# Two-layer graph attention on one core: layer 0 in a hand-made order, layer 1's rows turned by VectorE alone

## The chip, the cores and the metric

The kernel runs on one NeuronCore of a Trainium2 chip. The metric is the device time of one execution in microseconds (us); lower is better. The median of three runs of the kernel before is 937.08 us, from 936.54 to 939.74.

The names of the engines in the profile: PE is TensorE (PEld its weight loads), DVE is VectorE, ACT is ScalarE, POOL is GpSimd, SP is SyncE, which here only issues DMAs. An engine name with a q (SPq, ACTq) is that engine's sequencer issuing a DMA.

## What is computed

Two residual layers over 4096 nodes of 512 features, with a dense 4096 x 4096 adjacency matrix of positive weights (zero where there is no edge):

```python
# layer 0: attention inside graphs of 128 nodes (32 graphs); adj is both b and edge_encoding
h = relu(layernorm(x))
q, k, v = h @ Wq.T + bq, h @ Wk.T + bk, h @ Wv.T + bv
a = where(same_graph, q @ k.T / sqrt(512), 0)
scores = (a + adj + adj) * where(same_graph, 1, -1e6)
x = x + (softmax(scores) * same_graph) @ v

# layer 1: graph attention, 8 heads of 64, over all edges of adj
h = relu(layernorm(x))
mx = einsum('nf,hfd->hnd', h, W)
logits = (mx . a_origin)[:, :, None] + (mx . a_dst)[:, None, :]
attn = softmax(where(adj > 0, logits, -big))
x = x + concat_heads(attn @ mx)
```

In layer 1 the a_origin term cancels in the softmax, so a head's output is a sum over the neighbours of exp(t_j) * mx_j divided by the sum of exp(t_j). The kernel works on 32 tiles of 128 rows.

## The kernel before

It has four stages.

The start (`fold`) multiplies Wq and Wk into one matrix (`m_sb`), with the bias terms folded in: it loads and transposes both weights, spreads the biases with small matmuls, and forms the products.

Layer 0 goes through 16 groups of two tiles. Its loads of the adjacency matrix are half tiles of 1 MB in seven buffers; each half is turned into mask bytes by VectorE (stored in `a_d` for layer 1) and summed with exponentials by ScalarE. Eight tiles of layer 1 are projected in its gaps, with `prepare_on`:

```python
def begin1():                                  # a row tile of layer 1: load, normalise
    row = sb2.tile([P, D], F32, name="row1")
    nc.sync.dma_start(row, x1_d[len(rows1)])
    norm(row, row)
    rows1.append(row)

def turned1(row):                              # four TensorE transposes, relu out of PSUM
    hT = sb2.tile([P, KC, P], F32, name="hT1")
    relu_T(ps_t, row, hT)
    return hT
...
def relu_T(ps_pool, hn, dst):
    pt = ps_pool.tile([P, KC, P], F32, name="pt")
    for k in range(KC):
        nc.tensor.transpose(pt[:, k, :], hn[:, ts(k, P)], ident)
    nc.scalar.activation(dst, pt, AF.Relu)
...
for g in range(NG):                            # layer 0, cut
    ...
    s = scores(g, hT, gT, r, *look)
    prepare_on(last)
    if not last:
        ngT = queries(nhT)
    sT = turned(s)
    prepare_on(3 <= g and g % 2)
    ...
    for t in range(G):
        look_on(t)                             # adjacency halves of the next group
        if not last and t == 0:
            nvs.append(values(nhT, t))
        attend(sT, vs[t], g, t)
        if not last and t:
            nvs.append(values(nhT, t))
    ...
    if g + 2 < NG:
        nhT, hns = turned0(g + 2)
        nr = row_terms(hns)
```

The order on each engine is left to the framework in this stage. The lines of the profile in it: scores L519, queries L461, the turning of scores L538, values L473, attend L546 (with VectorE's x1, L548), transposes L136, projection of layer 1 L264, mask bytes L146, adjacency exponentials L496.

The middle stage projects layer 1's tiles 8 to 31, in an order that the program gives for all engines but TensorE. Tiles 8 to 15 are still turned by TensorE. Tiles 16 to 31 are turned by VectorE: a stream transpose turns 32 x 32 blocks, four tiles are collected in `blocks`, stored to DRAM and loaded back in another arrangement, which completes the turning:

```python
def turn(i):
    c, b = divmod(i, BY)
    if b == 0:
        blocks[c] = sb4.tile([P, P // B, KC, BY, B], F32, name="blocks")   # two buffers
    nc.vector.transpose(
        blocks[c][:, :, :, b], rows[i].rearrange("p (k q f) -> p q k f", k=KC, f=B)
    )
    if b == BY - 1:
        nc.sync.dma_start(hT_d[c], blocks[c].rearrange("p q k b r -> p q (k b r)"))

def move(c):
    hT = sb5.tile([P, P // B, KC, P], F32, name="hT4")
    for q in range(P // B):
        nc.sync.dma_start(hT[ts(q, B)]..., hT_d[c, :, q]...)
    for u in range(BY):
        hTs[c * BY + u] = hT[:, u]
```

The last stage (L315) sums, for each of the 32 tiles, over all neighbours: 96 matmuls of 128 x 128 by 348 columns for a tile. The change does not alter it.

Of the kernel before, what the change touches and what calls it, by code (L numbers as in the profile page):

```python
# [9 lines left out]
F32 = mybir.dt.float32  # L10
# [15 lines left out]
H = 8  # L26
# [18 lines left out]
MIXED = NT // 2  # L45
AHEAD = 8
# [7 lines left out]
def kernel(  # L54
# [43 lines left out]
    nc.scalar.dma_start(bq_sb, bq)  # L98
    bk_sb = const.tile([P, KC], F32, name="bk_sb")
    nc.scalar.dma_start(bk_sb, bk)  # L100
# [7 lines left out]
    def load_adj(pool, k):  # L108

        a = pool.tile([P, NH], F32, name="a")  # L110
        nc.sync.dma_start(a, adj[ts(k // 2, P), ts(k % 2, NH)])
        return a
# [26 lines left out]
    def mask_bytes(a8, a, h):  # L139

        half = ts(h, NW // 2)
        a8v = a8.rearrange("p (u c q b) -> p u c b q", c=NW, q=B, b=BY)[:, :, half]
        order = ("p (c b u q) -> p u c b q", "p (c u b q) -> p u c b q")[h]
        av = a.rearrange(order, c=NW // 2, b=BY, q=B)
        for u in range(P // B):
            nc.vector.tensor_scalar(  # L146
                a8v[:, u], av[:, u], 0.0, None, ALU.is_gt, saturate=False
            )
# [10 lines left out]
    def load_w1(pool, tmp):  # L159
# [3 lines left out]
        a_sb = tmp.tile([P, D], F32, name="a_sb", bufs=1)  # L163
        nc.sync.dma_start(a_sb, a_dst.to_broadcast([P, D]))
        for k in range(KC):
            wa = tmp.tile([P, D], F32, name="wa", bufs=1)
            nc.vector.tensor_tensor(wa, w[:, k, :D], a_sb, ALU.mult)
            nc.vector.tensor_reduce(
                w[:, k, D:], wa.rearrange("p (h d) -> p h d", d=HD), AX.X, ALU.add
            )  # L170
        return w

    def fold(sb, tmp, work, ps_t, ps_p, loads, first):
# [3 lines left out]
        wkT_sb = load_weight(tmp, wkT, "wkT_sb", KC, tag="lo")  # L177
        wqT_sb = load_weight(tmp, wqT, "wqT_sb", KC, tag="lo")
# [12 lines left out]

        nat = []
        for n, wT in enumerate((wkT_sb, wqT_sb)):
            w = tmp.tile([P, KC, D], F32, name=f"w{n}", tag="lo")
            for k in range(KC):
# [4 lines left out]
                if n == 0 and k == 0:  # L200
                    rows = [spread_bias(b) for b in (bk_sb, bq_sb)]
# [18 lines left out]
        for m in range(KC):  # L220
# [11 lines left out]
            if m == 3:  # L232
                first()
            pp = ps_p.tile([P, D], F32, name="pp")
            for k in range(KC):
                nc.tensor.matmul(
                    pp, wq[:, k, ts(m, P)], wk[:, k, :], start=(k == 0), stop=(k == KC - 1)
                )
            nc.scalar.mul(m_sb[:, m, :], pp, SCALE)  # L239
# [140 lines left out]
    with ExitStack() as straight:  # L380
# [4 lines left out]
        with ExitStack() as prep:  # L385
# [12 lines left out]
            rows1 = []  # L398

            def begin1():  # L400
                row = sb2.tile([P, D], F32, name="row1")
                nc.sync.dma_start(row, x1_d[len(rows1)])
                norm(row, row)
                rows1.append(row)

            def turned1(row):
                hT = sb2.tile([P, KC, P], F32, name="hT1")
                relu_T(ps_t, row, hT)
                return hT
# [13 lines left out]
            def prepare(i, hT, part):  # L423
                pm = project1(ps_p, hT, w1x)
                finish(weights(i, pm), pm, part)

            with (
                tc.tile_pool(name="adj0", bufs=AB, side="right") as ap,
# [4 lines left out]
                def turned0(g):  # L433

                    hT = sb.tile([P, KC, G * P], F32, name="hT")
                    hns = []
                    for t in range(G):
                        hn = sb.tile([P, D], F32, name="hn")
                        norm(xg[g][:, t, :], hn)
                        relu_T(ps_t, hn, hT[:, :, ts(t, P)])  # L440
                        hns.append(hn)
# [13 lines left out]
                def queries(hT):  # L455

                    gT = sb.tile([P, KC, G * P], F32, name="gT")
                    for m in range(KC):
# [8 lines left out]
                        )  # L467
                    return gT

                def values(hT, t):  # L470
# [6 lines left out]
                    nc.vector.tensor_add(v, pp, bv_sb)  # L477
                    return v

                def read(i, diag, sums):  # L480


                    a8 = sb.tile([P, N], FP8, name="a8", bufs=3)
                    n = 1
                    for h in range(2):
                        a, base = aa[2 * i + h], h * NH
                        mask_bytes(a8, a, h)
                        own = i * P - base
                        pieces = ((0, NH),)
                        if 0 <= own < NH:  # L490
                            nc.gpsimd.tensor_copy(diag, a[:, ds(own, P)])
                            pieces = ((0, own), (own + P, NH))
                        for c0, c1 in pieces:
                            if c0 < c1:
                                junk = sb.tile([P, NH], BF16, name="junk", bufs=1)
                                nc.scalar.activation(  # L496
                                    junk[:, c0:c1], a[:, c0:c1], AF.Exp, scale=2.0 * NEG,
                                    accum_out=sums[:, n : n + 1],
                                )
                                n += 1  # L500
                        if h:
                            nc.sync.dma_start(a_d[i], a8.bitcast(F32))
                        if 2 * i + h + AB < 2 * NT:
                            aa[2 * i + h + AB] = load_adj(ap, 2 * i + h + AB)
                    return n

                def seen():
                    return (
                        sb.tile([P, G, P], F32, name="diag", bufs=3),
# [4 lines left out]
                def scores(g, hT, gT, r, diag, sums, counts):  # L514
# [8 lines left out]
                    s = sb.tile([P, G, P], F32, name="s")  # L523
                    nc.vector.scalar_tensor_tensor(s, diag, 2.0, pss, ALU.mult, ALU.add)
                    for t in range(G):
# [3 lines left out]
                        )  # L529
                        rsum = rs_all[:, G * g + t : G * g + t + 1]  # L530
                        nc.vector.tensor_reduce(rsum, sums[t][:, : counts[t]], AX.X, ALU.add)
                        nc.vector.reciprocal(rsum, rsum)
                    return s

                def turned(s):
# [3 lines left out]
                    sT = sb.tile([P, G, P], F32, name="sT")  # L539
# [3 lines left out]
                def attend(sT, v, g, t):  # L543
                    i = G * g + t
                    po = ps_p.tile([P, D], F32, name="pp")
                    nc.tensor.matmul(po, sT[:, t, :], v, start=True, stop=True)  # L546
                    x1 = sb.tile([P, D], F32, name="x1")
# [12 lines left out]
                xg, aa = {}, {}  # L560
                first = []

                def loads():
                    load_pair(0)
                    first.append(load_weight(wp, wvT, "wv"))
                    nc.scalar.dma_start(bv_sb, bv.to_broadcast([P, D]))
                    for k in range(4):
                        aa[k] = load_adj(ap, k)
                    load_pair(1)
                    for k in range(4, AB):  # L570
                        aa[k] = load_adj(ap, k)

                m_sb, c_sb, u_sb, z_sb = fold(
                    wp, lo, sb, ps_t, ps_p, loads, lambda: first.extend(turned0(0))
                )
# [3 lines left out]
                look = seen()  # L579
                for t in range(G):  # L580
                    look[2].append(read(t, look[0][:, t, :], look[1][t]))
                gT = queries(hT)
                nhT, hns = turned0(1)
                nr = row_terms(hns)
                ahead = []
                for g in range(NG):
                    last = g + 1 == NG
                    if g + 2 < NG:
                        load_pair(g + 2)
                    if g == 1:  # L590
                        w1x = load_w1(pool1, sb)
                    nlook = seen()

                    def look_on(t):
                        if not last:
                            i = G * (g + 1) + t
                            nlook[2].append(read(i, nlook[0][:, t, :], nlook[1][t]))

                    def prepare_on(now):
                        if now:  # L600
                            i = len(ahead)
                            ahead.append(turned1(rows1[i]))
                            if i:
                                prepare(i - 1, ahead[i - 1], part_tile(lo, i - 1))

                    s = scores(g, hT, gT, r, *look)
                    prepare_on(last)
                    if last:
                        begin1()
                    if not last:  # L610
                        ngT = queries(nhT)
                    sT = turned(s)
                    prepare_on(3 <= g and g % 2)

                    for _ in range({2: 1, NG - 2: 1, NG - 1: 0}.get(g, int(3 <= g and g % 2))):
                        begin1()
                    nvs = []
                    for t in range(G):
                        look_on(t)
                        if not last and t == 0:  # L620
                            nvs.append(values(nhT, t))
                        attend(sT, vs[t], g, t)
                        prepare_on(last and t == 0)
                        if not last and t:
                            nvs.append(values(nhT, t))
                    if not last:
                        hT, r, gT, vs, look = nhT, nr, ngT, nvs, nlook
                    if g + 2 < NG:
                        nhT, hns = turned0(g + 2)
                        nr = row_terms(hns)  # L630

# [6 lines left out]
            sb5 = prep.enter_context(tc.tile_pool(name="sb5p", bufs=2, reuse_waits="tile"))  # L638
            begun = ExitStack()
            sb4 = begun.enter_context(  # L640
                tc.tile_pool(name="sb4p", bufs=2, side="right", reuse_waits="tile")
            )
            rows, of, blocks, hTs = {}, {}, {}, {}
# [469 lines left out]
```

## Time and profile before

| stage, us from the start | TensorE busy | VectorE busy | ScalarE busy | GpSimd busy | DMA engines' share |
|---|---|---|---|---|---|
| 0 to 29: start | 24.59 | 15.58 | 17.16 | 8.14 | 0.92 |
| 29 to 195: layer 0, first part | 165.78 | 125.98 | 113.99 | 38.00 | 0.93 |
| 195 to 212 | 16.86 | 10.88 | 9.95 | 4.93 | 0.93 |
| 212 to 340: layer 0, second part | 128.00 | 75.09 | 63.38 | 24.27 | 0.67 |
| 340 to 379: last group, first layer 1 tiles | 39.00 | 28.82 | 21.53 | 22.78 | 0.36 |
| 379 to 443: rest of the middle stage | 63.49 | 36.56 | 21.96 | 33.77 | 0.63 |
| 443 to 916: aggregation | 473.00 | 163.28 | 18.90 | 47.08 | 0.23 |
| 916 to 937: last tile and end | 15.15 | 6.04 | 1.25 | 1.48 | 0.14 |

A row is a stretch of the profiled execution, whose span is 936.6 us; each cell is how long the engine was busy in it. Matmuls are pipelined, so the profile's durations of single ones overlap; the time that a group of them takes is read from the start of the next group. Several DMA engines serve all queues; their share is the mean over 16.

### The profile page before, as it was taken

The numbers are of one execution on the slowest core, as the hardware profiler recorded it, in microseconds if no ns is written. First come the engines' busy times: TensorE is split into PE (matmuls) and PEld (weight loads), VectorE is DVE, ScalarE is ACT, GpSimd is POOL, SyncE is SP. The second block draws the span as 40 slices with busy tenths as digits, with TensorE's granted clock in tenths as the row PEclk, the third lists the DMA queues.
The fourth block names the chain that finished last, engine by engine and source line by source line (L and its number), as shares of the span: only waits on it lengthen the run. The fifth ranks groups of instructions, "written<-read, shape, count | busy, mean of one in ns | idle before, by whom it ended". The sixth has DMA issues, their size and how long they took to land.

```text
span 936.6 us, 13145 instructions
## 1 busy us (share of the span) xinstructions
PE 925.9 (99%) x4987; PEld 809.1 (86%) x4987; DVE 462.2 (49%) x992; ACT 268.1 (29%) x539; POOL 180.4 (19%) x344
## 2 busy tenths in 40 slices
PE   8999999999999999999999999999999999999997
PEld 5676677767677778888999999999999999999997
DVE  4678878777775447754463324242424233332412
ACT  4876576667672216532000000000000000000000
POOL 1311212331221116654101010110101010101010
PEclk9999999999999999999999999999999999999999
DMA  9999997989997114764123131312121222313111
GB/s 334 415 382 401 349 351 302 360 344 371 356 354 273 35 35 146 203 200 103 53 61 91 46 90 46 90 51 85 52 85 54 82 71 65 88 48 90 46 45 37
DMA packets 61062, 156.63 MB, mean 167 GB/s; under 512 B 6722, under 2 KB 23490, under 8 KB 52290
## 3 DMA queue, kind: packets, MB, share of 16 engines
q1 hardware_dynamic: 51058, 138.70, 42.9%
q10 hardware_dynamic: 9936, 17.05, 4.9%
q8 instruction: 40, 0.66, 0.3%
q14 instruction: 28, 0.23, 0.1%
HBM read 117.97 MB, written 37.75 MB: 166 GB/s over the span
## 4 chain that ended last, share of the span: by engine, by line
PE 94%; DMA 3%; ACT 2%; DVE 0%; SPq 0%; issue 0%; ACTq 0%
PE pg L315 51%; PE pp L264 12%; PE pp L461 11%; PE pp L473 11%; PE pp L546 3%; PE pss L519 3%; DMA a<-adj 2%; PE pt L136 2%; ACT junk L496 1%; PE pl L315 1%; DMA bv_sb<-bv 1%; PE pss L538 0%; ACT m_sb L239 0%; ACT gT L465 0%; DVE x L548 0%
## 5 line engine op out<-in xcount | busy, mean ns | idle before, releaser
L315 PE MATMUL pg<-part,ata 128*128 128x348 f32 (+1 forms) x1536 | 246.7, 321 | 0.0
L315 PEld LDWEIGHTS pg<-part,ata 128*128 128x128 f32 x1536 | 244.5, 188 | 0.1
L315 PE MATMUL pg<-part,atb 128*128 128x348 f32 x1472 | 236.4, 321 | 0.0
L315 PEld LDWEIGHTS pg<-part,atb 128*128 128x128 f32 x1472 | 234.2, 188 | 0.1
L329 ACT COPY tot<-pg 128x522 f32<-128x522 f32 x31 | 18.6, 600 | 453.4 <-PE pg L315 453.4
L496 ACT ACTIVATE junk<-a 128x2048 bf16<-128x2048 f32 (+15 forms) x92 | 124.5, 1353 | 36.3 <-DMA a<-adj 15.1
L264 PE MATMUL pp<-w1x,hT 128*128 128x256 f32 (+1 forms) x512 | 114.9, 383 | 0.5 <-DVE e L273 0.5
L473 PE MATMUL pp<-wv,hT 128*128 128x512 f32 x256 | 115.0, 593 | 0.3 <-ACT hT L137 0.3
L461 PE MATMUL pp<-hT,m_sb 128*128 128x256 f32 x512 | 113.2, 379 | 0.0
L301 DVE CAST atb<-at 128x4096 fp32r<-128x4096 fp8e4 x16 | 36.7, 2293 | 152.2 <-PE pg L315 152.2
L264 PEld LDWEIGHTS pp<-w1x,hT 128*128 128x128 f32 x512 | 96.0, 190 | 15.0 <-issue 0.9
L461 PEld LDWEIGHTS pp<-hT,m_sb 128*128 128x128 f32 x512 | 96.1, 190 | 12.9 <-issue 0.5
L301 DVE CAST ata<-at 128x4096 fp32r<-128x4096 fp8e4 (+1 forms) x17 | 36.8, 2167 | 140.4 <-PE pg L315 140.3
L146 DVE TENSOR_SCALAR a<-a 128x512 fp8e4<-128x512 f32 x256 | 96.8, 457 | 5.7 <-DMA a_d<-a 5.7
L473 PEld LDWEIGHTS pp<-wv,hT 128*128 128x128 f32 x256 | 47.8, 190 | 54.9 <-issue 53.1
L767 POOL COPY den_all<-tot 128x1 f32<-128x1 f32 x31 | 5.8, 186 | 365.0 <-DVE tot L330 365.0
L771 POOL TENSOR_TENSOR tot<-tot,row 128x512 f32<-128x512 f32 x31 | 39.9, 1288 | 62.2 <-DVE tot L335 58.1
L248 POOL TENSOR_TENSOR part<-e,part 128x522 fp32r<-128x522 f32 x32 | 41.1, 1285 | 12.9 <-ACT part L245 12.7
L122 POOL TENSOR_SCALAR ve<-mv 128x1 f32<-128x1 f32 x64 | 16.3, 259 | 131.1 <-DVE mv L120 131.0
L137 ACT ACTIVATE hT<-pt 128x512 f32<-128x512 f32 x48 | 26.9, 596 | 50.8 <-PE pt L136 40.5
L477 DVE TENSOR_TENSOR v<-pp,bv_sb 128x512 f32<-128x512 f32 x32 | 22.0, 687 | 39.2 <-PE pp L473 39.2
L292 DVE STREAM_TRANSPOSE at<-mw 128x1024 f32<-128x1024 f32 x32 | 39.6, 1238 | 2.1 <-DMA mw<-a_d 2.1
(113 smaller groups left out, 698.4 us busy)
## 6 DMA issues: line engine op xcount, KB each, us to landing
a<-adj SPq DMA_DIRECT2D x64, 1024.0 KB, 12.2
a_d<-a SPq DMA_DIRECT2D x32, 512.0 KB, 10.3
mw<-a_d SPq DMA_DIRECT2D x128, 128.0 KB, 3.9
row<-x_d SPq DMA_DIRECT2D x41, 256.0 KB, 3.5
xg<-x SPq DMA_DIRECT2D x16, 512.0 KB, 5.1
x_d<-x ACTq DMA_DIRECT2D x32, 256.0 KB, 4.3
out<-tot ACTq DMA_DIRECT2D x31, 256.0 KB, 3.7
rowm<-x_d SPq DMA_DIRECT2D x16, 256.0 KB, 5.2
```

Source lines behind the costliest of these rows:

```text
L146: nc.vector.tensor_scalar(a8v[:, u], av[:, u], 0.0, None, ALU.is_gt, saturate=False)
L248: nc.gpsimd.tensor_sub(dst[:, :, 1, :], e3, dst[:, :, 0, :].bitcast(F32))
L264: nc.tensor.matmul(pm[g][:, :n], hT[:, k, :], w1x[:, k, g * HW : g * HW + n], start=(k == 0), stop=(k == KC - 1),)
L292: nc.vector.transpose(at8.rearrange("p c n b -> p (c n b)").bitcast(F32).rearrange("p (c u n) -> p c u n", c=NW, n=B), mw.rearrange("p u ( ...
L301: nc.vector.tensor_copy(at[:, c0 * BY : c1 * BY].rearrange("p (c b) q -> p c b q", b=BY), at8[:, c0:c1].rearrange("p c q b -> p c b q"),)
L315: nc.tensor.matmul(pg[:, : 2 * CW1].rearrange("p (s w) -> p s w", s=2)[:, :, :n], at[:, j, :], part(j)[:, c, :, :n], start=(j == 0), stop= ...
L461: nc.tensor.matmul(pp[:, : G * P], m_sb[:, k, ts(m, P)], hT[:, k, :], start=(k == 0), stop=(k == KC - 1),)
L473: nc.tensor.matmul(pp, hT[:, k, ts(t, P)], wv[:, k, :], start=(k == 0), stop=(k == KC - 1))
L496: nc.scalar.activation(junk[:, c0:c1], a[:, c0:c1], AF.Exp, scale=2.0 * NEG, accum_out=sums[:, n : n + 1],)
L519: nc.tensor.matmul(pss[:, t, :], gT[:, k, ts(t, P)], hT[:, k, ts(t, P)], start=(k == 0), stop=(k == KC - 1),)
L546: nc.tensor.matmul(po, sT[:, t, :], v, start=True, stop=True)
L771: nc.gpsimd.tensor_add(num, num, row)
```

## The change

It has three purposes. TensorE no longer turns any row of layer 1: tiles 0 to 15 are turned by VectorE as tiles 16 to 31 were, inside layer 0's groups, each one group after its row was fetched. With 16 tiles to be turned in there, layer 0's order is now given by the program on all five engines. And at the start the bias loads are put behind the first weight on one queue, with ten transposes of the identity ahead of the first real work to warm TensorE up.

SBUF has no room for more buffers. In layer 0, `blocks` has one buffer (in the pool `keep`), and the buffer for the returned rows (`hT4`) alternates with one of the seven adjacency buffers (tag `"a"`). Two lines of the loop look ahead: `fetch(g)` loads row tile g, and tile g - 1 (`mine`) is normalised and turned in group g.

The diff, cut to its core (moved and renamed parts, and the branch for general inputs that isn't taken, are left out):

```diff
-MIXED = NT // 2
-AHEAD = 8
+AHEAD = 9
+WARM = 10
...
-    nc.scalar.dma_start(bq_sb, bq)
-    nc.scalar.dma_start(bk_sb, bk)
...  (in fold)
         wkT_sb = load_weight(tmp, wkT, "wkT_sb", KC, tag="lo")
+        nc.sync.dma_start(bk_sb, bk)
+        nc.sync.dma_start(bq_sb, bq)
         wqT_sb = load_weight(tmp, wqT, "wqT_sb", KC, tag="lo")
         loads()
...
+        pt = ps_t.tile([P, KC, P], F32, name="pt")
+        for _ in range(WARM):
+            nc.tensor.transpose(pt[:, 0, :], ident, ident)
...
-                if n == 0 and k == 0:
+                if n == 0 and k == KC - 1:
                     rows = [spread_bias(b) for b in (bk_sb, bq_sb)]
...
+            keep = prep.enter_context(
+                tc.tile_pool(name="keep", bufs=1, side="right", reuse_waits="tile")
+            )
+            def turn(i, row, pool):
+                c, b = divmod(i, BY)
+                if b == 0:
+                    blocks[c] = pool.tile([P, P // B, KC, BY, B], F32, name="blocks")
+                nc.vector.transpose(
+                    blocks[c][:, :, :, b], row.rearrange("p (k q f) -> p q k f", k=KC, f=B)
+                )
+            def store(c):
+                nc.sync.dma_start(hT_d[c], blocks[c].rearrange("p q k b r -> p q (k b r)"))
+            def move(c):
+                hT = keep.tile(
+                    [P, P // B, KC, P], F32, name="hT4", tag="a" if c and c % 2 == 0 else "hT4"
+                )
...
+            def relu1(i):
+                norm(rows[i], rows[i], of[i])
+                nc.scalar.activation(rows[i], rows[i], AF.Relu)
...  (in loads)
-                    nc.scalar.dma_start(bv_sb, bv.to_broadcast([P, D]))
+                    nc.sync.dma_start(bv_sb, bv.to_broadcast([P, D]))
...  (in the products of fold)
+                def between(m, after):
+                    if m == 2 and not after:
+                        first.append(normed0(0))
+                        read(0, 0, look)
+                    if m == 3 and not after:
+                        first.extend(turned0(0, first.pop()))
+                    if m == 3 and after:
+                        read(1, 1, look)
...  (layer 0)
+                with tc.manual_schedule(engines={E.PE, E.DVE, E.Activation, E.Pool, E.SP}):
+                    for g in range(NG - 1):
+                        new = G * (g + 1)
+                        mine = g - 1
+                        if g + 2 < NG:
+                            load_pair(g + 2)
+                        if g == 1:
+                            fetch(0)
+                            w1x, dots = load_w1(pool1, sb2, tag="e")
+                        if g in (6, 11, 14):
+                            move((6, 11, 14).index(g))
+                        nlook = seen()
+                        def look_on(t, h):
+                            sum_half(new + t, h, nlook[0][:, t, :], nlook[1][t], nlook[2])
+                        def between(m):              # after the m-th quarter of the queries
+                            if m < 2:
+                                mask_half(new, m)
+                                look_on(0, m)
+                            if m == 1:
+                                store_mask(new)
+                                row_sums(g, *look)
+                                if g > 1:
+                                    of[mine] = moments(rows[mine])
+                                mask_half(new + 1, 0)
+                            if m == 2 and g > 1:
+                                relu1(mine)
+                        s = scores(hT, gT, rs[g], *look)
+                        ngT = queries(nhT, between)
+                        sT = turned(s)
+                        if g + 2 < NG:
+                            ofs = [moments(xg[g + 2][:, t, :]) for t in range(G)]
+                        look_on(1, 0)
+                        mask_half(new + 1, 1)
+                        rest = prepare() if g in (7, 8, 9, 10, 13) else None
+                        look_on(1, 1)
+                        store_mask(new + 1)
+                        if g:
+                            fetch(g)
+                        if g in (5, 9, 13):
+                            store(g // BY - 1)
+                        if g + 2 < NG:
+                            hns = normed0(g + 2, ofs)
+                        if g > 1:
+                            turn(mine, rows[mine], keep)
+                        if 2 <= g < 2 + KC:
+                            dots(g - 2)
+                        v0 = values(nhT, 0, later=True)
+                        nvs = []
+                        if rest:
+                            rest()
+                        attend(sT, vs[0], g, 0, lambda: nvs.append(v0()))
+                        attend(sT, vs[1], g, 1)
+                        if g + 2 < NG:
+                            rs[g + 2] = row_terms(hns)
+                        nvs.append(values(nhT, 1))
+                        ...
+                        if g + 2 < NG:
+                            nhT, hns = turned0(g + 2, hns)
...  (the last group holds the other three projections: tiles 5 to 7; then the middle stage)
-                    if i + 1 < MIXED:
-                        hTs[i + 1] = sb2.tile([P, KC, P], F32, name="hT1")
-                        relu_T(ps_t, rows[i + 1], hTs[i + 1])
+                    if far <= NT:
+                        turn(far - 1, rows[far - 1], (keep, sb4)[(far - 1) // BY % 2])
+                        if far % BY == 0:
+                            store(far // BY - 1)
```

`sum_half` holds the exponentials and the diagonal of one adjacency half, and issues the load of the half seven later; `attend` ends with ScalarE issuing the store of x1; `prepare` projects a tile and returns what weighs it.

## The prediction

> **What bounds the kernel now.** I read the page's first part for the busiest engine, then the chain that ended last in order of time, then the TensorE timeline of the start, and last the issues of the DMA queues. The page of the kernel before gives busy time and share of the span by engine:
>
> ```profile
> PE 925.9 (99%) x4987; PEld 809.1 (86%) x4987; DVE 462.2 (49%) x992; ACT 268.1 (29%) x539; POOL 180.4 (19%) x344
> ```
>
> TensorE is idle for 936.6 - 925.9 = 10.7 us in all: 3.9 before its first instruction, 5.4 after its last, about 1.4 between. So only three things can gain: fewer TensorE instructions, an earlier start, a shorter tail. The chain (start, us, what) for one iteration of layer 0 (a group of two tiles), and then for one layer 1 tile below 16:
>
> ```profile
> 118.07 1.79 PE pss L519 x16
> 119.86 6.91 PE pp L461 x32
> 126.77 0.22 PE pss L538 x2
> 126.98 3.44 PE pp L473 x8
> 130.42 1.72 PE pp L546 x4
> 132.13 3.43 PE pp L473 x8
> 135.57 0.87 PE pt L136 x8
> ...
> 363.06 0.44 PE pt L136 x4
> 363.50 3.51 PE pp L264 x16
> ```
>
> A group is 18.37 us without a gap: scores, queries, turned, values, two attends, values, the next rows' transposes. A layer 1 tile costs 0.44 of transposes (L136) and 3.51 of projection (L264). The TensorE timeline of the start (start, us, then what it ran and waited for):
>
> ```profile
> 3.92 1.08 PE L198 MATMUL pt<-ident,wkT_sb 128*128 128x128 f32 x4 [3.92 <-DMA wkT_sb<-wkT]
> 4.80 1.91 PE L184 MATMUL pp<-ident,bk_sb 128*128 128x128 f32 x8
> 6.51 1.91 PE L184 MATMUL pp<-ident,bq_sb 128*128 128x128 f32 x8
> 8.21 2.00 PE L198 MATMUL pt<-ident,wkT_sb 128*128 128x128 f32 x12
> 10.12 2.63 PE L198 MATMUL pt<-ident,wqT_sb 128*128 128x128 f32 x16
> 12.59 7.03 PE L236 MATMUL pp<-w,w 128*128 128x512 f32 x16
> ```
>
> The bias matmuls fill 4.80 to 8.21 while three quarters of wkT are still on their way (7.1 us from issue to landing, issued from 0.85 on); the weight products start at 12.59 and the first values at 29.23. Lastly the DMA issues (KB each, median us to landing) and VectorE's turning of a row (busy, mean ns, idle before):
>
> ```profile
> a<-adj SPq DMA_DIRECT2D x64, 1024.0 KB, 12.2
> a_d<-a SPq DMA_DIRECT2D x32, 512.0 KB, 10.3
> hT_d<-blocks SPq DMA_DIRECT2D x4, 1024.0 KB, 4.6
> L655 DVE STREAM_TRANSPOSE blocks<-rowm 128x512 f32<-128x512 f32 x10 | 7.0, 700 | 3.5 <-ACT rowm L730 3.4
> ```
>
> A store of turned rows lands in 4.6 us in the quiet middle stage; inside layer 0, where the DMA engines are 77 to 100% busy, even half its bytes take 10.3.
>
> **What the Trainium skill says.** "TensorE: Matmul & The Clock Gate", section "Part 1: The HAM clock gate", says that TensorE runs at half its clock until it has been busy for some 3.4 us, and falls back after about as long idle. The trace agrees with the first half: eight bias matmuls take 1.70 us at the start, eight of the same shape 0.89 at 19.46. No idle stretch here is long enough to show the second. The same page, "Part 4: PE-mode transpose", says transposes don't count as busy for that clock; no run shows it yet, and it casts doubt on the ten warm-up transposes. "DMA: Bandwidth & Descriptors", section "Issuing engines are not separate DMA queues", says DMAs of all engines share the same 16 and interleave; the landing times above agree. "Trainium Kernel Development and Optimization", section "Best Practices", has "Double-buffer for performance"; the buffer of turned rows inside layer 0 is single after the change.
>
> **The change part by part.**
> 1. *Transposes removed.* Layer 1's tiles 0 to 15 no longer go through TensorE: 16 x 0.44 = 7.0 us, all on the chain. Their 16 evacuations on ScalarE (596 ns each) become 16 relus of 530 ns; VectorE gains 16 x 0.70 = 11 us, beside other work.
> 2. *Start.* Bias loads behind wkT on the same queue, bias matmuls after wkT's last piece, bv's broadcast behind wv. The transposes of wkT can follow its landing (by about 6 instead of 8.2), then ScalarE's evacuations pace the rest: ten copies of 0.59 to 0.65 from 4.8 on end at 11 rather than 13.4. I put the products at 10.1 instead of 12.59. After them 32 products x 0.43 + 1.1 + 0.87 = 15.7 end near 26, where the first values could begin instead of at 29.23, because ScalarE's relus of the first rows then stand behind two exponentials instead of the five of the trace. If the warm-up fails, 1.6 us of it is lost again in the bias matmuls. Estimate: 2.5 gained.
> 3. *Middle stage.* One stall around 412.7 to 414.8 (0.5 us of idle TensorE) should go with AHEAD 9; tiles 8 to 31 are then 24 x 3.51. VectorE per tile: statistics 0.87, turn 0.70, weigh 0.82, norm 0.55 = 2.9 of 3.5. It fits. Estimate: 0.5 gained.
> 4. *Aggregation* (473 us) and tail: the same instructions, 0.
>
> So TensorE alone would end at 937.1 - 7.0 - 2.5 - 0.5 = 927.
>
> 5. *VectorE inside a group.* Per group it has now: 13.9 (126.0 busy in the 166 us from 29 to 195, by 18.37) + statistics 0.85 + norm 0.55 + turn 0.70 = 16.0, and 1.36 more in groups 2 to 5 for w1's dot products. Under 18.37, so it fits, in strict order, with 1 to 2 us to spare.
> 6. *The stores of turned rows.* In groups 5, 9 and 13, `store` of a full block is issued, and right after it `turn` begins the next block in the same single buffer, so VectorE must wait until the store has landed. I lay a group out from the start of its scores. ScalarE: two score exponentials to 3.7; then in order 4 gT (0.47 each), 4 adjacency exponentials (2.1 each, 0.3 more for the split one), relu, sT: the fourth ends at 15.3. SyncE's last adjacency load waits for that one, and the mask store, a row fetch and the block store follow at 0.4 each: issued at 16.5, though VectorE reaches `turn` at 12.9. Ahead of it in the queues stand 1.05 + 0.52 + 0.26 MB, with itself 2.9 MB; at the 400 GB/s seen in full stretches 7.2 us, and something for the landing: about 24.3.
>  - Group 5: then turn 0.7, dots 1.36, v 0.69, two x1 1.5; ScalarE, whose in-order stream waits for x1 to issue its store, does 0.4 of issue and 1.2 of relus. The next queries start at 30.3 instead of 20.2: 10 us lost.
>  - Group 9 holds a projection (TensorE 21.9 long). Its second attend reuses the PSUM buffer that `weigh` frees, and `weigh` follows `turn`: 24.3 + 1.6 = 25.9 instead of 16.8: 9 lost.
>  - Group 13: no more loads to wait for; issue near 13, landing 19.5, the attend at 21.1 instead of 16.8: 4 lost.
>  - Gaps of 9 us may cool the clock: two times about 1.7 us at half speed, 3 more.
>
> Sum of part 6: up to 26 us, against 10 gained: 953 if everything in it happens as laid out. A landing 2 us sooner takes 6 off: 947.
>
> **The rivals.**
> - *No stall, TensorE's sum holds*: 925 to 931. For it: TensorE idles 1.4 us in all between its first and last instruction now, adjacency loads have seven buffers (1.75 groups ahead), and an order made by hand was presumably looked at with its waits. Against it: I can find nothing in the order that hides the landing of those three stores.
> - *The stores stall the in-order engines*, as in part 6: 940 to 957. For it: the buffer is single, the store stands directly ahead of its overwriting, no mask store inside layer 0 landed in under 6.1 us. Against it: the store may be issued sooner than I lay out, and I may misjudge how much slack VectorE has.
> - *DMA becomes the bound of layer 0*: a group moves 6.3 MB now (342 GB/s at 18.37 us); fetches add 0.26, stores and returns of turned rows 0.63 on average: 7.2 MB, 391 GB/s, at the edge of the 384 to 430 seen. Groups with a projection (328) and seven buffers give slack. It would add 0 to 6 us, and lengthen the landings of part 6.
> - *VectorE falls behind in groups 2 to 5* (17.4 of 18.37): 0 to 4 us.
>
> **Range and chances.** I give the no-stall case 0.3 (centre 928) and the stalls 0.7 (centre 949, give or take 7). The median of the mixture is near 944; 923 to 958 should hold it 8 times in 10. Faster by over 2% means under 918.3: more than TensorE's own sum can give, 0.03. Slower by over 2% means over 955.8: the full stalls plus a cold clock or a DMA bound, 0.14. The rest, 0.83.
>
> **What would show it.** Part 1: transposes on rows of layer 1 gone from TensorE, its busy time down by about 7. Part 2: L236's successor at 10 instead of 12.6 and first values at 26. Part 3: layer 1's projections back to back. Part 6: in the waits, VectorE's stream transposes waiting for the DMA hT_d<-blocks, three times some 7 to 11 us, and three gaps of TensorE at the ends of groups 5, 9 and 13. If those waits are under 3 us, or TensorE runs through them, part 6 is wrong and the time is about 927. If layer 0 is long but the waits are on adjacency loads, the DMA rival holds.

## The result, and the profile after

The changed kernel takes 981.67 us (median of six runs, 980.58 to 983.54) against 937.15 for the kernel before: a ratio of 1.0473, 95% interval 1.0456 to 1.0490. The change costs 44.5 us; the prediction had 944 and a range up to 958.

The first part of the changed kernel's page, and the TensorE clock row of its second part (40 equal slices, in tenths of full clock):

```profile
PE 933.7 (95%) x4933; PEld 810.1 (83%) x4933; DVE 476.9 (49%) x1016; ACT 260.8 (27%) x507; POOL 185.3 (19%) x344
...
PEclk9999998899799989899999999999999999999999
```

TensorE runs 54 instructions fewer (64 transposes gone, ten warm-up transposes added) and is yet busy 7.8 us longer, because its clock fell in some slices; and it is idle for 47 us of the span instead of 10.7. So of the 44.5 us, 36.7 are more idle time and 7.8 more busy time.

The stretch from the scores of one group to those of the next, from TensorE's timeline, in us. "Own work" is what the group's TensorE instructions take at full clock: 18.37, or 21.88 with a projection, or 17.50 for group 14, which has no next rows to turn:

| group | 0, 1, 3, 7, 8, 10, 11, 12, 14 | 2 | 4 | 5 | 6 | 9 | 13 |
|---|---|---|---|---|---|---|---|
| own work | as measured | 18.37 | 18.37 | 18.37 | 18.37 | 21.88 | 21.88 |
| measured | as own work | 22.42 | 19.89 | 20.10 | 34.61 | 35.94 | 30.62 |
| lost | 0 | 4.1 | 1.5 | 1.7 | 16.2 | 14.1 | 8.7 |

The sum of the losses is 46.3. The whole difference is then: the first scores start 2.5 sooner (41.50 instead of 43.98); from there to the last group's scores 338.6 instead of 295.5, so 43.1 more; from there to the first aggregation matmul 106.5 instead of 103.7, 2.8 more; the rest 1.1 more. That is 44.5.

The waits of the changed kernel (engine, tile and line, what it waited for: us in total, times, longest us):

```profile
DVE blocks L415 <- DMA hT_d<-blocks: 33.2, 4, 13.6
...
DVE stats L117 <- DMA row<-x_d: 22.8, 11, 4.3
...
ACT hT L136 <- DVE x L612: 19.9, 2, 16.8
...
PE pp L609 <- DVE e L280: 16.6, 2, 10.7
PE pp L504 <- ACT hT L136: 16.4, 3, 14.0
```

The first line is the wait that the prediction named: the next turn waits for the store of the full block. It waits 13.60 us in group 5, 13.03 in group 9 and 5.63 in group 13, where 7 to 11 each were expected; the fourth time is 0.90 us in the middle stage. The third and fifth carry the first of these on to TensorE in group 6's queries (L504), by way of ScalarE's stream, which is in order; the fourth does so in the second attend of groups 9 and 13 (L609). The second line the prediction didn't have: VectorE waits eleven times for a row of layer 1, six of them (13.7 us) for the rows that `fetch` loads.

The chain that ended last, in order of time, from group 4's end to group 6's queries (start, us, what):

```profile
137.78 10.85 DMA row<-x_d
148.66 0.71 DVE stats L117
...
157.41 0.42 SPq L556
157.89 0.50 SPq L439
158.44 10.88 DMA hT_d<-blocks
169.41 0.71 DVE blocks L415
...
172.01 1.33 DVE x L612 x2
173.80 1.09 ACT hT L136 x2
174.94 9.19 PE pp L504 x32
```

Two transfers of nearly 11 us stand one behind the other. The first is the row for group 5, fetched at the end of group 4 and needed early in group 5 (which starts at 138.93). Its lateness pushes ScalarE's exponentials (behind the row's relu in its order) back, SyncE's mask store and row fetch (L556, L439) behind them, and with those the block store. VectorE's turn at 169.41 is 30.5 us into the group. The queries then take 9.19 us, not 6.91: the clock is low.

### The profile page after: what moved, and what is told of

Read it like the earlier page. It is cut to its first block, busy times and chain, and to the rows that moved or that the text cites. A ratio compares the mean times of both kernels' runs of the same rounds, so it can differ in the third digit from the quotient of the medians.

```text
span 981.1 us, 13043 instructions
## 1 busy us (share of the span) xinstructions
PE 933.7 (95%) x4933; PEld 810.1 (83%) x4933; DVE 476.9 (49%) x1016; ACT 260.8 (27%) x507; POOL 185.3 (19%) x344
## 4 chain that ended last, share of the span: by engine, by line
PE 76%; DMA 12%; DVE 4%; ACT 3%; issue 2%; POOL 2%; SPq 1%; ACTq 0%; DVEq 0%
PE pg L322 49%; PE pp L271 9%; DMA row<-x_d 6%; PE pp L517 6%; PE pp L504 5%; DMA hT_d<-blocks 3%; PE pss L578 2%; ACT junk L547 2%; PE pp L609 1%; PE pp L242 1%; POOL ve L121 1%; PE pl L322 1%; POOL rstd L123 1%; DMA a<-adj 1%; DVE stats L117 1%
## 5 line engine op out<-in xcount | busy, mean ns | idle before, releaser
L504 PE MATMUL pp<-hT,m_sb 128*128 128x256 f32 x512 | 117.2, 388 | 16.4 <-ACT hT L136 16.4
L504 PEld LDWEIGHTS pp<-hT,m_sb 128*128 128x128 f32 x512 | 98.7, 195 | 30.9 <-ACT hT L136 16.9
L271 PE MATMUL pp<-w1x,hT 128*128 128x256 f32 (+1 forms) x512 | 117.5, 391 | 4.0 <-DVE e L280 2.0
L517 PE MATMUL pp<-wv,hT 128*128 128x512 f32 x256 | 118.8, 609 | 0.0
L271 PEld LDWEIGHTS pp<-w1x,hT 128*128 128x128 f32 x512 | 98.7, 194 | 21.1 <-issue 3.1
L308 DVE CAST atb<-at 128x4096 fp32r<-128x4096 fp8e4 x16 | 36.7, 2294 | 152.6 <-PE pg L322 152.6
L308 DVE CAST ata<-at 128x4096 fp32r<-128x4096 fp8e4 (+1 forms) x17 | 36.8, 2168 | 140.5 <-PE pg L322 140.4
L144 DVE TENSOR_SCALAR a<-a 128x512 fp8e4<-128x512 f32 x256 | 91.6, 445 | 0.3 <-DMA a<-adj 0.3
L121 POOL TENSOR_SCALAR ve<-mv 128x1 f32<-128x1 f32 x64 | 38.4, 599 | 174.5 <-DVE mv L119 174.5
L123 POOL TENSOR_TENSOR rstd<-ve,neghalf 128x1 f32<-128x1 f32 x64 | 53.1, 829 | 5.5
L609 PE MATMUL pp<-v,sT 128*128 128x512 f32 x64 | 33.0, 631 | 18.7 <-DVE e L280 16.6
L609 PEld LDWEIGHTS pp<-v,sT 128*128 128x128 f32 x64 | 12.5, 201 | 34.7 <-DVE e L280 18.5
## 6 DMA issues: line engine op xcount, KB each, us to landing
xg<-x SPq DMA_DIRECT2D x16, 512.0 KB, 10.9
```

The lines of the kernel that those rows point to most:

```text
L121: nc.gpsimd.tensor_scalar(ve, mv[:, 1:2], EPS, None, ALU.add)
L123: nc.gpsimd.tensor_tensor(rstd, ve, neghalf, ALU.pow)
L144: nc.vector.tensor_scalar(a8v[:, u], av[:, u], 0.0, None, ALU.is_gt, saturate=False)
L271: nc.tensor.matmul(pm[g][:, :n], hT[:, k, :], w1x[:, k, g * HW : g * HW + n], start=(k == 0), stop=(k == KC - 1),)
L308: nc.vector.tensor_copy(at[:, c0 * BY : c1 * BY].rearrange("p (c b) q -> p c b q", b=BY), at8[:, c0:c1].rearrange("p c q b -> p c b q"),)
L504: nc.tensor.matmul(pp[:, : G * P], m_sb[:, k, ts(m, P)], hT[:, k, :], start=(k == 0), stop=(k == KC - 1),)
```

## The experiments

Theory 1: the wait for the late store, through the single buffer, is most of the loss. Theory 2: the late fetch is the root, and the store only suffers from it. Rivals: DMA bandwidth, or a VectorE that is too full in a strict order. The first three runs set these apart.

**e1: the block's store one group sooner.**

```diff
-                        if g in (5, 9, 13):
-                            store(g // BY - 1)
...
                         if g > 1:
                             turn(mine, rows[mine], keep)
+                        if g in (4, 8, 12):
+                            store(g // BY - 1)
```

> Theory 1: the overwriting of the single buffer of turned rows waits for a store issued just ahead of it; that costs 16 + 14 + 9 = 39 us in groups 5, 9 and 13. With the store issued one group sooner, right behind the turn that fills the block, these go, and the row fetches still make some groups 1 to 2 us too long: about 950 us. Theory 2, the late row fetch is the root and the store only suffers from it: 975 or more. Rival, DMA bandwidth bounds layer 0: the same bytes move, so within 5 us of 981.7.

Measured: 953.12 us (952.30 to 954.54), 28.6 less. VectorE's waits for the block store fall from 33.2 to 2.6; those for rows rise:

```profile
DVE stats L117 <- DMA row<-x_d: 34.1, 11, 5.6
...
DVE blocks L415 <- DMA hT_d<-blocks: 2.6, 1, 2.6
```

The same bytes move, so DMA bandwidth is not the cause.

**e2: the row fetch at the head of its group, the store still late.**

```diff
+                        if g:
+                            fetch(g)
                         if g in (6, 11, 14):
                             move((6, 11, 14).index(g))
...
-                        if g:
-                            fetch(g)
```

> The row fetch goes to the head of its group instead of its end; the stores stay late. Theory 1: the store is issued some 3 us sooner in each of groups 5, 9 and 13 and the 3 us lost in groups 4 and 5 go: about 970 us. Theory 2 (the fetch is the root): 945 or less. DMA bound: within 5 us of 981.7.

Measured: 971.25 us (969.64 to 973.14), 10.4 less. Groups 4 and 5 are back at 18.37, and the loss of group 13 falls from 8.7 to 4.0. The store's wait stays:

```profile
DVE blocks L415 <- DMA hT_d<-blocks: 32.5, 4, 14.3
```

The store of group 5 is issued at 15.5 us of its group instead of 19.5. Theory 2 falls: the fetch is a quarter of the loss, not its root.

**e3: both.**

> Store and fetch both early. Theory 1 with the fetch as a lesser cost: layer 0 loses only the 4 us in front of group 2: 981.7 - 42 = about 939 us. DMA bound or VectorE too full in strict order: over 960.

Measured: 944.88 us (943.67 to 946.09), 36.8 less, nearly the sum of the two (39.0). 6 us more than expected remain: group 7 is 2.0 too long and group 6 0.9, and the last group and the middle stage still hold gaps. DMA bandwidth and a full VectorE would have left it above 960; both fall.

**e7 and e8: is it the buffer?** A second buffer for turned rows fits only if one adjacency buffer goes, so e7 is the changed kernel with six of them, and e8 has the second buffer besides, with the late store left alone.

```diff
-AB = 7
+AB = 6
...  (e8 alone; the last group's two turns likewise)
-                            turn(mine, rows[mine], keep)
+                            turn(mine, rows[mine], (keep, sb)[mine // BY % 2])
```

> The changed kernel with six adjacency buffers instead of seven, as the control for the next: a little later loads, 980 to 988 us. If adjacency landing bounds layer 0: over 990.

> As e7, with a second buffer for turned rows inside layer 0, the store still late. If the wait is for the buffer and not for the store's place in the queue: e7 less some 29 us, as e1 gained. If the late store costs in another way (it delays the loads behind it): within 5 us of e7.

Measured: e7 983.03 us (982.59 to 984.44), e8 957.05 (955.63 to 958.83): 26.0 less. A second buffer does what the early store does, to within 3 us, with the store still late (issued 19.7 us into group 5), and no wait of VectorE for a block's store is left. So what waits is the overwriting, and what costs the time is a single buffer together with a store placed just ahead of it; either can be mended. One adjacency buffer fewer makes no difference that these runs can tell (ratio to the kernel before 1.0495, 1.0478 to 1.0512, against 1.0473, 1.0456 to 1.0490): adjacency landing doesn't bound layer 0 of the changed kernel. Whether six would do where layer 0 runs without these stalls is not shown.

**a1: layer 0's order left to the framework**, with all else of the change.

```diff
-                with tc.manual_schedule(engines={E.PE, E.DVE, E.Activation, E.Pool, E.SP}):
+                if True:
                     for g in range(NG - 1):
```

> The changed kernel with layer 0's order left to the framework on all engines, the middle stage's kept. If the loss is due to places in the hand-made order (late store, late fetch) and the framework issues both when they are ready: 940 to 955 us. If it is due to the work itself (16 more turns on VectorE, more DMA) whatever the order: 970 or more.

Measured: 948.50 us (947.31 to 950.67). So 33 us of the 44.5 belong to the hand-made order, and the added work isn't the bulk of the loss. VectorE doesn't wait for a block's store inside layer 0 here. The remaining 11.5 us over the kernel before are this order's own gaps and the added work together, not taken apart; the longest gap of TensorE in layer 0 is 3.22 us, for a normalised row of x.

**e4, e5, e6, e9, e10: the other gaps.** Starting from e3, each was read from the profile of the one before.

e4 (its diff on top of e3, cut): layer 1's first row is turned behind group 3's transposes; the first block of the middle stage has a buffer of its own; the return of block 3 stands behind more row loads; the last group's first x1 ahead of the last row's norm.

```diff
-                        if g == 1:
-                            of[0] = moments(rows[0])
-                            relu1(0)
-                            turn(0, rows[0], keep)
...
                             nhT, hns = turned0(g + 2, hns)
+                        if g == 1:
+                            of[0] = moments(rows[0])
+                            relu1(0)
+                            turn(0, rows[0], keep)
...
-                        turn(far - 1, rows[far - 1], (keep, sb4)[(far - 1) // BY % 2])
+                        turn(far - 1, rows[far - 1], (sb4, keep)[(far - 1) // BY % 2])
```

> As e3, and: layer 1's first row is turned behind the transposes of group 3's rows (4 us in front of group 2), the first block of the middle stage has a buffer of its own, the return of block 3 stands behind two more row loads, and x1 of the last group's first tile stands ahead of the last row's norm (8 us lost around 390 to 411). If those gaps are what they look like in the profile: about 928 us, TensorE's own sum. If they only move: 935 to 940.

Measured: 938.89 us (937.26 to 944.07), 6.0 less than e3 but 12 over TensorE's own sum. Group 2 is at 18.37; in the last group TensorE now waited 3.4 us for x1.

e5: layer 0 and the middle stage in one order, and w1's dot products behind both x1.

> As e4, with layer 0 and the middle stage in one hand-made order (in e4 VectorE's first work of the middle stage still ran ahead of the last group's x1, and TensorE waited 3.4 us for it), and w1's dot products behind both x1 instead of ahead of them. If those two gaps are what is left: 938.9 - 3.4 - 1.6 (colder clock) - 1.4 = about 932 us, under the kernel before. If they move: 937 to 940.

Measured: 941.51 us (939.79 to 943.89): slower than e4. The last group's gap only moved: the middle stage's first row loads now stood behind block 3's store on SyncE, and TensorE waited 3.8 us for what came of it. That alone hardly makes it slower: from the last group's scores to the aggregation it is 0.3 us longer than in e4. What is longer in the profiled execution is group 7, 6.9 us over its own work where e4 lost 0.7. The chain there runs through two loads of x (12.92 and 5.30 us to landing). e6, with the same order, lost 1.4 there, so this varies, and why is open.

e6: e5 without warm-up transposes.

> As e5 without the ten warm-up transposes. If transposes warm the clock: the first transposes and bias matmuls run at half speed for longer, 1 to 2 us slower than e5. If transposes don't count as busy[...]: within 0.5 us of e5.

Measured: 938.48 us (935.88 to 944.89). The products of the weights start at 10.80 us instead of 11.05 in e5. The ten transposes gain nothing, so the expectation of 1 to 2 us was wrong; the other, within 0.5, isn't met either, but the 3 us between the two medians lie in later groups (group 7 above all) and the runs overlap.

e9: e6 with block 3's store behind the first three row loads.

> As e6, with the fourth block's store behind the first three row loads of the middle stage. In e6 and e5 those loads stood behind that store on SyncE, VectorE waited 5.4 us for them and TensorE 3.7 us. If that gap goes: 938.5 - 3.7 - 1.5 (colder clock) = about 933 us, under the kernel before. If it only moves: 937 to 939.

Measured: 937.13 us (933.45 to 941.16), ratio to the kernel before 1.0002 (0.9988 to 1.0017). 1.4 us less than e6, a quarter of what was expected and not clear of noise (e6's ratio is 1.0019, 1.0007 to 1.0032). TensorE's wait in the profile shrinks from 3.7 to 2.1 us.

e10: e9 with the next rows' statistics behind the last mask bytes, and their norm behind the turn (the first of the two is shown).

```diff
-                        if g + 2 < NG:
-                            ofs = [moments(xg[g + 2][:, t, :]) for t in range(G)]
                         look_on(1, 0)
                         mask_half(new + 1, 1)
+                        if g + 2 < NG:
+                            ofs = [moments(xg[g + 2][:, t, :]) for t in range(G)]
```

> As e9, with the statistics of the next rows of x behind the last mask bytes of the group, and their norm behind the turn: VectorE waited 20 us in all for these rows' landing in e5, of which 2 to 5 us reached TensorE. If that is left: e9 less 2, about 931 us. If VectorE has the slack already: equal to e9 within 1 us.

Measured: 932.78 us (931.10 to 936.22), ratio 0.9955 (0.9937 to 0.9972): 0.45% faster than the kernel before, and clear of e9's 1.0002. VectorE's wait for the rows of x falls from 15.4 us in e9 to 11.8 here:

```profile
DVE stats L117 <- DMA xg<-x: 11.8, 6, 4.8
```

Groups 0 to 6 are all at 18.37, but they are so in e9 too. Of the 2.7 us between the two profiled executions, 1.1 lie ahead of the first scores, where the edit changes nothing, and 0.8 in the groups (group 7 loses 1.2 instead of 1.8). So how much of the 4.4 us between the medians the edit itself is worth is not shown. The first part of e10's page:

```profile
PE 918.7 (99%) x4923; PEld 803.1 (86%) x4923; DVE 475.8 (51%) x1016; ACT 260.9 (28%) x507; POOL 173.2 (19%) x344
```

TensorE runs 64 instructions fewer than in the kernel before, the four transposes of each of 16 tiles. It is busy 7.2 us less. That this is near the 7.0 of part 1 is partly luck: the start is 2.2 us less busy, and slow clock behind a gap in the middle stage takes 1.7 of that back.

**b1: the start's loads alone in the kernel before**: bias loads behind wkT, bv behind wv, the bias matmuls behind wkT's last piece, no warm-up.

> The kernel before with the bias loads behind wkT, bv behind wv and the bias matmuls behind wkT's last piece; no warm-up, no hand-made order. If the 2.5 us gained at the start come from the loads' order: 934.5. If they need ScalarE's order (relus ahead of the exponentials of the second tile): 936 to 937.5.

Measured: 938.12 us (937.63 to 941.08), ratio 1.0015 (1.0007 to 1.0024). The products start at 10.80 instead of 12.59, but the first values only at 28.34 instead of 29.23, since products wait 1.6 us for an evacuation behind the exponentials; the first scores start at 42.98. So the loads' order brings 1.0 of the 2.5 us; that ScalarE's order brings the rest fits this wait, but was not tested alone. Even the 1.0 is not in the total: from the first scores to the last group's the profiled execution takes 296.9 us, where the kernel before took 295.5.

## Why the prediction was wrong, point by point

The mechanism of part 6 was right: the turns of groups 5, 9 and 13 wait for the store of the one buffer. Two steps failed. The largest is the size of part 6, 26 us predicted and 39 measured. The other is the "it fits" of part 5, which left out that rows land late; this also fed the first.

1. *Transposes removed, 7.0 us*: right as far as the runs show. The 64 instructions are gone in e10 and its busy time is 7.2 us down, with the reservation made there; in the changed kernel it is buried.
2. *Start, 2.5 us*: right in size (the first scores at 41.50 instead of 43.98). The first values begin at 26.85, predicted near 26, and the products at 11.12, predicted 10.1. The warm-up brings nothing, and not for the reason suspected (last section).
3. *Middle stage, 0.5 gained*: wrong. From the last group's scores to the aggregation it is 2.8 us slower, though ten tiles' transposes (4.4 us) are gone from it. The prediction counted VectorE's work per tile and did not lay out the last group, where x1, block 3's store and the first rows of the middle stage follow each other. In the trace TensorE waits there for x1 (2.02 us) and again behind those rows (2.03), with half clock after each.
4. *Aggregation and tail, 0*: 1.1 us slower; the cause is open.
5. *VectorE inside a group, "it fits"*: this step failed. Its work does fit (a group without projection takes 18.37 where nothing is late), but the step added up durations and asked for no landing. The row for `moments(mine)` is fetched at the end of the group before, which part 6 itself put at about 16.1 us of that group. With the 10 us that mask stores took to land, the row is there at about 26.1 - 18.4 = 7.7 us of the next, where the order asks for it at about 6. In the trace it was 9.7 us in group 5. This loop from fetch through statistics and exponentials to the next fetch took 19 to 21 us a turn (the chain's row transfers start at 116.46, 137.78 and, behind it, 157.89), longer than a group's own work. It cost 3.2 us of TensorE in groups 4 and 5 and made the stores of groups 5 and 13 later; with the fetch at the head of the group (e2) the whole gain is 10.4.
6. *The stores*: the mechanism was right, with its three places and both ways to TensorE (ScalarE's relus behind x1; the PSUM buffer behind `weigh`). The size was not, and this is the term most mis-sized: 10 + 9 + 4 + 3 for the clock = 26 predicted, 16.2 + 14.1 + 8.7 = 39 measured. Of the 39, TensorE is idle for 13.95 + 10.71 + 5.89 = 30.5, where 23 were predicted, and 8.5 are instructions run at a slow clock (2.29, 3.35 and 2.85), where 3 were. For group 5: issue at 19.5 us instead of 16.5 (the row loop); landing after 10.9 instead of 7.8. In group 9 the issue is at 16.6, as laid out, and the landing at 26.5 instead of 24.3. While these two stores were under way the DMA engines moved 315 and 328 GB/s, not the 400 reckoned with. In group 13 the issue is at 16.1, not 13: the row fetched at the end of group 12 lands at 8.6 us of the group, and the mask bytes, the mask store and the block store follow it in their orders.
7. *Group 2*: 4.1 us that no part had, layer 1's first row turned ahead of group 3's relus in ScalarE's order.

With the full stalls the prediction stood at 953. Missing were 13 in the stores' size, 7.3 in the row loop and group 2, 7.7 in the last group and the middle stage (2.8 lost where the working had 4.9 of gain left), and 1.1 in the tail: 982. The prediction then took its centre down to 944 because it gave three chances in ten to an order without stalls, on no evidence of the profile: "presumably looked at with its waits". That hedge took 9 us off. Without it the prediction would have missed by 29 us all the same.

Of the rivals: DMA as the bound falls with e1 and e3 (the landing under load still sets the length of the waits), a full VectorE with e3, and no stall with the waits.

## What to carry to other kernels

In a hand-made order, adding up an engine's durations says whether the work fits, not whether it flows. For each transfer write down when it is issued (behind what on its queue), when it lands under that stage's load, and when its reader asks for it; and look for loops through two engines and a transfer, whose length sets the pace even when every engine has slack. A buffer with one copy should be emptied as soon as it is full: the same store, one group sooner, was worth 28.6 us here. And count the slow clock after each gap: it was 8.5 us on top of 30.5 of idle time.

## What the runs showed of the hardware that was not expected

A gap of TensorE of some 2 us can be enough to halve its clock. Busy time of each engine (TensorE, its weight loads, VectorE, ScalarE, GpSimd), clock, DMA share and GB/s of the changed kernel around a gap of 2.10 us (80.19 to 82.29):

```profile
80.00:82.00 2.00, 0.20 (x2) 0.00 (x1) 1.24 (x3) 1.36 (x3) 0.27 (x2) 1.00 1.03 425
82.00:84.00 2.00, 1.71 (x7) 1.49 (x8) 2.00 (x8) 1.12 (x5) 0.00 (x0) 0.87 1.01 414
84.00:86.00 2.00, 2.00 (x6) 1.57 (x5) 1.45 (x8) 1.02 (x2) 0.00 (x0) 0.50 1.03 404
86.00:88.00 2.00, 2.00 (x9) 1.67 (x8) 0.93 (x3) 1.80 (x5) 0.00 (x0) 0.78 0.40 146
```

The number before the DMA share is the clock: 0.87 and 0.78 are means over slices that it spent partly at 0.50, so it was at half from some 1.2 us after work had resumed, for about 3.4. The queries took 1.8 us longer for it. Gaps of 2.02 and 2.03 us did the same later in the changed kernel (work resumed at 393.93 and 411.02), and so did one of 3.42 (e4) and those of 5.89 to 13.95 behind the stores. One of 1.35 (e4) did not, but neither did one of 3.46 in e3, where 144 matmuls then took 0.22 us each, full clock:

```profile
372.13 31.80 PE L271 MATMUL pp<-w1x,hT 128*128 128x264 f32 x144 [3.46 <-DVE e L280]
```

So length alone doesn't decide. The Trainium skill, "TensorE: Matmul & The Clock Gate", section "Part 1: The HAM clock gate", speaks of an idle window of about 3.4 us; here less than two thirds of that sufficed three times. Where it happens, a gap of 2 us costs nearly twice itself.

Transposes do warm the clock here. The clock column of the profile reads 1.00 all through the start, so the clock is judged by durations. Start of e6, which has no warm-up (TensorE's timeline):

```profile
3.66 3.11 PE L205 MATMUL pt<-ident,wkT_sb 128*128 128x128 f32 x12 [3.66 <-DMA wkT_sb<-wkT]
6.56 0.58 PE L187 MATMUL pp<-ident,bk_sb 128*128 128x128 f32 x2
6.98 0.60 PE L205 MATMUL pt<-ident,wkT_sb 128*128 128x128 f32 x4
7.41 0.83 PE L187 MATMUL pp<-ident,bk_sb 128*128 128x128 f32 x6
```

The two matmuls at 6.56 take 0.21 us each, the four transposes at 6.98 take 0.11: full clock, 3.3 us after the first transpose, with nothing but transposes and two matmuls run. In e5, with its ten warm-up transposes from 1.52 on, nothing but transposes ran ahead of these four, which take 0.66 us, near the 0.60 above and not the 1.08 of the four at the start of the kernel before:

```profile
5.83 0.66 PE L205 MATMUL pt<-ident,wkT_sb 128*128 128x128 f32 x4 [0.21 <-DMA wkT_sb<-wkT]
```

The Trainium skill, same page, "Part 4: PE-mode transpose", says that transposes don't count as busy; these float32 ones did, if they ran in the mode that the page means, which the trace doesn't say. Why the warm-up gains nothing all the same is not isolated. In e6, without it, the products still start 0.25 us sooner than in e5, so the clock of the first transposes isn't what holds them up.
